# Five graphs in flight, and a layer norm whose division is moved behind the product

## The chip, the cores and the metric

One core of a Trainium2 chip runs the whole program. The metric is the device time of one launch in microseconds (us), lower is better. The runs of one kernel mostly lie within 0.3% of each other.

In this kernel TensorE multiplies and transposes matrices and writes to the memory PSUM; VectorE and ScalarE take the products out of PSUM (an eviction) and work on the memory SBUF, where GpSimd does some additions and powers too. In the lines of the profile they are PE, DVE, ACT and POOL; PEld is TensorE's loading of weights. The granted clock is the share of TensorE's full clock that the trace records.

## The reference

64 independent graphs, each with 256 nodes of 512 features and a 256x256 adjacency matrix, go through four layers. Every layer begins with the same normalisation:

```
def _layernorm(x, axis=-1, eps=1e-5):
    m = jnp.mean(x, axis=axis, keepdims=True)
    v = jnp.var(x, axis=axis, keepdims=True)
    return (x - m) / jnp.sqrt(v + eps)
# --- layer 0 (adj_preln) ---
h = jnp.maximum(_layernorm(x, axis=-1), 0.0)
x = x + _L0_gnn_ref(h, adj, L0_gnn_W_qk, L0_gnn_W_v)
# ... layers 1, 2 and 3 in the same form
```

Layer 0 multiplies h with a query/key matrix (512x128) and a value matrix (512x512). Layer 1 is a graph attention with eight heads and a masked softmax. Layer 2 is a tanh attention with eight heads. Layer 3 multiplies with a query/key matrix (512x1024), a value matrix (512x512) and the adjacency. All in float32.

The row's factor 1/sqrt(v + eps) is positive, so relu(r (x - m)) = r relu(x - m), and a product of the rows can be multiplied by r afterwards. That identity is what half of the change uses.

## The kernel before

The kernel describes each graph as some 75 tasks: what they wait for, how long each engine is estimated to need, which buffers they take and give. A planner, run once in Python while the program is built, repeatedly picks the task that could start first by its estimates and writes its instructions. So every engine's order of instructions is fixed before the chip starts. The framework below it may put instructions of one task between those of another. What the traces then show on the chip is each engine waiting for another one or for a DMA (TensorE's waits are listed in the prediction).

```
IN_FLIGHT = 4
BEHIND = 30.0
...
    def ready(self, task, ends): ...       # the estimated time at which inputs and buffers are there
    def issue(self, task, g, at):
        task.run(*[t[2] for t in passing])
        for engine, length in task.steps:
            start = max(at, self.free[engine])
            self.free[engine] = start + length
            at = start + length + (0.25 if engine == "PE" else 0.12)
    def run(self, graph, count):
        ...
                        start = max(at, self.free.get(engine, 0.0))
                        key = (round(start, 2), g.b * BEHIND - task.rest)   # the smallest is next
```

`BEHIND` weighs the number of a graph against the work that it still has to do: it decides between tasks that could start at the same time. The normalisation before:

```
@task(f"stats{layer}", after, [("V", 1.9), ("G", 0.75)])
def _():
    ...bn_stats, bn_aggr of both chunks of 128 rows...
    nc.vector.tensor_scalar(rstd, mv[:, :, 1], EPS, None, op0=OP.add)
    nc.gpsimd.tensor_tensor(rstd, rstd, power, OP.pow)
@task(f"hn{layer}", f"stats{layer}", [("V", 1.1)], {"hn": 1})
def _():
    for c in range(NC):
        nc.vector.tensor_scalar(g["hn"][:, c, :], g["xt"][:, c, :], st["mv"][:, c, 0:1],
                                st["rstd"][:, c:c + 1], op0=OP.subtract, op1=OP.mult)
# then TensorE turns each chunk, ScalarE takes it out of PSUM with a relu ("ht"), and products follow
```

In layer 1 GpSimd adds a mask to the scores of two heads (2.4 us each, 256 of them), while VectorE finds masked maxima:

```
nc.gpsimd.tensor_tensor(e, e, g["negt"][:, None].to_broadcast([P, 2, NC, N]), OP.add)
```

## Time and profile before

| | before |
|---|---|
| median time | 4856.3 us |
| TensorE / VectorE / ScalarE / GpSimd busy | 92 / 63 / 35 / 25% |
| TensorE idle, sum of the gaps ahead of its matmuls | 379 us |
| mean granted clock of TensorE | 0.961 |
| DMA share | 0.18 |

The busy shares say where the time can be won at most: only TensorE is near its limit. (The prediction speaks of 386 us of idle time: the span less the busy time. The sum of the gaps ahead of matmuls leaves out what lies after the last one, hence 379.) The waits of TensorE say what it stood for. The lines are shown in the prediction.

### The profile page before, as it was taken

The page shows a single profiled execution, that of the slowest core. Times are in us where ns is not written, and L with a number is a line of the kernel's source. Part 1 is how long each engine was busy: PE and PEld are TensorE (multiplying, and loading weights), DVE is VectorE, ACT ScalarE, POOL GpSimd, SP SyncE. Part 2 cuts the span into 40 slices and gives each one's busy share as a digit, 9 for nine tenths or more (in the row PEclk, how much of TensorE's full clock was granted, in tenths as well). Part 3 has the DMA queues.
Part 4 walks back from the last instruction along what each step waited for, and adds up shares of the span by engine and source line. Part 5 has one row for each costly group of instructions (what it writes and reads, how often), then busy time and mean ns, then how long its engine had stood idle before and what let it go on. Part 6 is the DMA issues. An engine that isn't in the chain of part 4 may idle for free.

```text
span 4848.4 us, 60906 instructions
## 1 busy us (share of the span) xinstructions
PE 4462.3 (92%) x22850; PEld 3051.0 (63%) x22850; DVE 3042.9 (63%) x7530; ACT 1679.2 (35%) x3333; POOL 1203.2 (25%) x969
## 2 busy tenths in 40 slices
PE   6799999999999999999999999999999999999998
PEld 4566666666666666666666656666666666566665
DVE  5666665666566656656666666566567656665664
ACT  1333333343343333333333333333334333333332
POOL 1231222222222212222222222122222222221220
PEclk9889999999999999999999999999999999999999
DMA  4211111111121111111111211111111112111110
GB/s 118 77 53 60 65 68 60 65 68 54 62 77 51 65 60 64 68 59 63 70 52 64 77 51 65 60 65 68 60 65 68 55 61 77 50 65 60 65 55 22
DMA packets 107975, 306.89 MB, mean 63 GB/s; under 512 B 18016, under 2 KB 48800, under 8 KB 83104
## 3 DMA queue, kind: packets, MB, share of 16 engines
q1 hardware_dynamic: 92160, 295.21, 16.9%
q10 hardware_dynamic: 15520, 7.80, 0.6%
q8 instruction: 179, 2.93, 0.3%
q14 instruction: 116, 0.95, 0.1%
HBM read 267.85 MB, written 35.13 MB: 62 GB/s over the span
## 4 chain that ended last, share of the span: by engine, by line
PE 73%; DVE 12%; issue 6%; POOL 6%; ACT 2%; DMA 1%; ACTq 0%; POOLq 0%; DVEq 0%; SPq 0%
PE tr L296 17%; PE acc L296 15%; PE acc L538 9%; PE tr L655 8%; PE tr L605 5%; PE acc L626 5%; DVE junk L477 4%; PE tr L365 4%; PE tr L677 4%; POOL pair L513 4%; PE tr L589 3%; DVE pair L608 1%; DVE hn L357 1%; PE tr L408 1%; PE tr L574 1%
## 5 line engine op out<-in xcount | busy, mean ns | idle before, releaser
L296 PE MATMUL acc<-wv_s,ht 128*128 128x512 f32 x2048 | 990.4, 627 | 31.0 <-ACT ht L366 30.8
L513 POOL TENSOR_TENSOR pair<-pair,negt 128x1024 f32<-128x1024 f32 x256 | 622.6, 2448 | 213.4 <-ACT pair L511 212.2
L296 PEld LDWEIGHTS acc<-wv_s,ht 128*128 128x128 f32 x2048 | 395.1, 203 | 436.0 <-issue 393.9
L366 ACT ACTIVATE ht<-tr 128x512 f32<-128x512 f32 x512 | 292.5, 594 | 1043.7 <-PE tr L365 940.4
L477 DVE CUSTOM_DVE_ANT_0 junk<-all,neg 128x256 f32<-128x256 f32 x1024 | 605.8, 629 | 16.7 <-DMA all<-er_d 15.8
L351 POOL TENSOR_TENSOR rstd<-rstd,power 128x2 f32<-128x2 f32 x256 | 213.1, 834 | 1326.9 <-DVE rstd L350 1026.8
L538 PEld LDWEIGHTS acc<-feats,pair 128*128 128x128 f32 x4096 | 492.4, 196 | 62.8 <-issue 48.5
L538 PE MATMUL acc<-feats,pair 128*128 128x65 f32 x4096 | 514.4, 280 | 10.7 <-ACT pair L521 10.6
L357 DVE TENSOR_SCALAR hn<-xt,mv,rstd 128x512 f32<-128x512 f32 x512 | 446.7, 900 | 110.0 <-POOL rstd L351 94.5
L549 POOL TENSOR_TENSOR xt<-xt,o 128x256 f32<-128x256 f32 x256 | 190.3, 752 | 1275.3 <-DVE o L547 1178.5
L365 PE MATMUL tr<-ident,hn 128*128 128x128 f32 x2048 | 319.7, 292 | 187.7 <-DVE feats L461 87.3
L609 ACT ACTIVATE pair<-pair 128x512 f32<-128x512 f32 x512 | 311.5, 628 | 521.1 <-DVE pair L608 520.6
L608 DVE TENSOR_TENSOR pair<-tr,at 128x512 f32<-128x512 f32 x512 | 330.9, 685 | 238.4 <-PE tr L605 231.9
L655 PE MATMUL tr<-ht,m_s 128*128 128x256 f32 x2048 | 469.3, 384 | 0.0
L296 PE MATMUL tr<-w_s,ht 128*128 128x512 f32 x1024 | 460.8, 595 | 0.8 <-ACT ht L366 0.7
L655 PEld LDWEIGHTS tr<-ht,m_s 128*128 128x128 f32 x2048 | 391.2, 193 | 84.2 <-issue 30.0
L511 ACT ACTIVATE pair<-all,ec 128x256 f32<-128x256 f32 x1024 | 426.3, 498 | 31.8 <-PE acc L538 11.8
L365 PEld LDWEIGHTS tr<-ident,hn 128*128 128x128 f32 x2048 | 252.2, 151 | 250.6 <-DVE feats L461 89.9
L521 ACT ACTIVATE pair<-pair 128x1024 f32<-128x1024 f32 x256 | 268.0, 1057 | 352.4 <-DVE pair L519 258.1
L565 DVE TENSOR_TENSOR xp<-tr,b_bc 128x512 f32<-128x512 f32 x128 | 88.2, 689 | 440.7 <-PE tr L296 440.4
L346 DVE BATCH_NORM_STATS2 stats<-xt 128x6 f32<-128x512 f32 x512 | 336.8, 677 | 16.4 <-DMA xt<-in_x_dram 10.1
L605 PE MATMUL tr<-xc,xpt 64*128 64x256 f32 x2048 | 323.3, 403 | 4.0 <-DVE xc L591 1.7
(87 smaller groups left out, 5502.0 us busy)
## 6 DMA issues: line engine op xcount, KB each, us to landing
all<-er_d SPq DMA_DIRECT2D x128, 1024.0 KB
all<-m_d SPq DMA_DIRECT2D x64, 1024.0 KB
xt<-in_x_dram SPq DMA_DIRECT2D x64, 512.0 KB
out_dram<-xt SPq DMA_DIRECT2D x64, 512.0 KB
adj<-in_adj_dram SPq DMA_DIRECT2D x64, 256.0 KB
mask_in<-in_nodemask_dram SPq DMA_DIRECT2D x64, 128.0 KB
w_n<-in_L_gnn_Wqk_dram ACTq DMA_DIRECT2D x16, 128.0 KB
wv_s<-in_L_gnn_W_v_dram ACTq DMA_DIRECT2D x1, 1024.0 KB
```

What stands on the lines that cost most here:

```text
L296: nc.tensor.matmul(p, ht[:, k, c * P:(c + 1) * P], w[:, k], start=(k == 0), stop=(k == KC - 1))
L346: nc.vector.bn_stats(stats[:, c, :], xt[:, c, :])
L357: nc.vector.tensor_scalar(g["hn"][:, c, :], g["xt"][:, c, :], st["mv"][:, c, 0:1], st["rstd"][:, c:c + 1], op0=OP.subtract, op1=OP.mult)
L365: nc.tensor.transpose(pt[:, k * P:(k + 1) * P], g["hn"][:, c, k * P:(k + 1) * P], ident)
L477: nc.vector.tensor_tensor_reduce(junk, g["all:en"][:, h, :], g["neg"][:, c, :], 1.0, -BIG, OP.add, OP.max, st["mx"][:, c, h:h + 1])
L511: nc.scalar.activation(e[:, s, j, :], g["all:es"][:, h, :], AF.Prelu, bias=st["ec"][:, j, H + h:H + h + 1], alpha=0.2)
L513: nc.gpsimd.tensor_tensor(e, e, g["negt"][:, None].to_broadcast([P, 2, NC, N]), OP.add)
L538: nc.tensor.matmul(po[i][:, h % 4, :], e[:, s, j, i * P:(i + 1) * P], feats[:, j, h, :], start=(j == 0), stop=(j == NC - 1))
L605: nc.tensor.matmul(ps[s][:, m, :], g["xpt"][half, p, m * P:(m + 1) * P], g["xc"][half, p, :], start=True, stop=True)
L608: nc.vector.tensor_tensor(th[:, s], ps[s], g["at"], OP.mult)
L609: nc.scalar.activation(th[:, s], th[:, s], AF.Tanh)
L655: nc.tensor.matmul(pz[:, s, :], m3_s[:, k, d * P:(d + 1) * P], g["ht"][:, k, :], start=(k == 0), stop=(k == KC - 1))
```

## The change

The intent: give TensorE more graphs to choose from, and shorten the chain at the head of layers 0 to 2. The statistics, the power and the normalisation are no longer in a row: a chunk is centred right after its own statistics, and the deviation divides where the products leave PSUM. To find room for a fifth graph, the adjacency has three buffers instead of four and is loaded a second time for layer 3; its transpose has five instead of four. One more constant is moved, `BEHIND` from 30 to 20.

```
-IN_FLIGHT = 4
-BEHIND = 30.0
+IN_FLIGHT = 5
+BEHIND = 20.0
-ADJ_BUFS = 4
-AT_BUFS = 4
+ADJ_BUFS = 3
+AT_BUFS = 5
...
+            late_scale = layer < 3
+            def centred(c):
+                @task(f"hn{layer}{c}", (after if late_scale else f"rstd{layer}") + ...,
+                      [("V", 1.39 if late_scale else 0.55)], {} if c else {"hn": 1})
+                def _():
+                    if late_scale:
+                        stats(c)
+                    nc.vector.tensor_scalar(g["hn"][:, c, :], g["xt"][:, c, :], mv[:, c, 0:1],
+                                            None if late_scale else st["rstd3"][:, c:c + 1], op0=OP.subtract,
+                                            **({} if late_scale else {"op1": OP.mult}))
...
-                nc.vector.tensor_copy(g["qk"][:, c, :], pq[:, :2 * A0])
+                nc.vector.tensor_scalar(g["qk"][:, c, :], pq[:, :2 * A0], st["rstd0"][:, c:c + 1], None,
+                                        op0=OP.mult)
...
-                nc.vector.tensor_tensor(g["xp"][:, c, :], pf, b2_bc, OP.add)
+                nc.vector.scalar_tensor_tensor(g["xp"][:, c, :], pf, st["rstd2"][:, c:c + 1], b2_bc,
+                                               op0=OP.mult, op1=OP.add)
... (layer 1's evictions and layer 0's weights in the same way)
-        @task("neg", "fa0", [("G", 0.7)], {"neg": 1})
+        @task("neg", "load <at", [("G", 0.7)], {"neg": 1}, {"adj": (1, 2)})
...
+        @task("again", "y0", [("D", 4.0)], {"adj": 1})
+        def _():
+            nc.sync.dma_start(g["adj"], adj[b].rearrange("(c p) m -> p c m", p=P))
```

More of the change, by code (lines that the diff above doesn't have):

```diff
@@ L328, in _ @@
             nc.sync.dma_start(g["adj"], adj[b].rearrange("(c p) m -> p c m", p=P))
-        @task("at", "load", [("PE", 0.45), ("A", 0.6)], {"at": 1}, banks=1)
+        @task("at", "load", [("PE", 0.45), ("A", 0.6)], {"at": 1}, {"adj": (1, 2)}, banks=1)
         def _(pa):
@@ L338, in normed @@
         def normed(layer, after):
-            @task(f"stats{layer}", after, [("V", 1.9), ("G", 0.75)])
-            def _():
-                xt = g["xt"]
-                stats = small.tile([P, NC, 6], F32, name="stats")
-                mv = small.tile([P, NC, 2], F32, name="mv")
-                for c in range(NC):
-                    nc.vector.bn_stats(stats[:, c, :], xt[:, c, :])
-                for c in range(NC):
-                    nc.vector.bn_aggr(mv[:, c, :], stats[:, c, :])
-                rstd = small.tile([P, NC], F32, name="rstd")
-                nc.vector.tensor_scalar(rstd, mv[:, :, 1], EPS, None, op0=OP.add)
-                nc.gpsimd.tensor_tensor(rstd, rstd, power, OP.pow)
-                st["mv"], st["rstd"] = mv, rstd
@@ L354, in _ @@
-            @task(f"hn{layer}", f"stats{layer}", [("V", 1.1)], {"hn": 1})
-            def _():
-                for c in range(NC):
-                    nc.vector.tensor_scalar(g["hn"][:, c, :], g["xt"][:, c, :], st["mv"][:, c, 0:1],
-                                            st["rstd"][:, c:c + 1], op0=OP.subtract, op1=OP.mult)
+            late_scale = layer < 3
+            def centred(c):
+                @task(f"hn{layer}{c}", (after if late_scale else f"rstd{layer}") + (f" <hn{layer}0" if c else ""),
+                      [("V", 1.39 if late_scale else 0.55)], {} if c else {"hn": 1})
+                def _():
+                    if late_scale:
+                        stats(c)
+                    mv = st[f"mv{layer}"]
+                    nc.vector.tensor_scalar(g["hn"][:, c, :], g["xt"][:, c, :], mv[:, c, 0:1],
+                                            None if late_scale else st["rstd3"][:, c:c + 1], op0=OP.subtract,
+                                            **({} if late_scale else {"op1": OP.mult}))
@@ new lines, in stats, with root @@
+            def stats(c):
+                if not c:
+                    st[f"mv{layer}"] = small.tile([P, NC, 2], F32, name="mv")
+                six = small.tile([P, 6], F32, name="six")
+                nc.vector.bn_stats(six, g["xt"][:, c, :])
+                nc.vector.bn_aggr(st[f"mv{layer}"][:, c, :], six)
+            def root():
+                st[f"rstd{layer}"] = rstd = small.tile([P, NC], F32, name="rstd")
+                nc.vector.tensor_scalar(rstd, st[f"mv{layer}"][:, :, 1], EPS, None, op0=OP.add)
+                nc.gpsimd.tensor_tensor(rstd, rstd, power, OP.pow)
@@ L360, in turned @@
+            if late_scale:
+                for c in range(NC):
+                    centred(c)
+                task(f"rstd{layer}", f"hn{layer}0 hn{layer}1", [("V", 0.18), ("G", 0.75)])(root)
+            else:
+                @task(f"rstd{layer}", after, [("V", 1.9), ("G", 0.75)])
+                def _():
+                    for c in range(NC):
+                        stats(c)
+                    root()
+                for c in range(NC):
+                    centred(c)
             def turned(c):
-                @task(f"ht{layer}{c}", f"hn{layer}" + (f" <ht{layer}0" if c else ""), [("PE", 0.5), ("A", 0.6)],
+                @task(f"ht{layer}{c}", f"hn{layer}{c}" + (f" <ht{layer}0" if c else ""), [("PE", 0.5), ("A", 0.6)],
@@ L380, in weighted @@
                 value(c)
-            @task(f"soft{layer}", after, [("PE", 0.25), ("V", 0.42), ("A", 1.0), ("V", 0.4)], banks=1)
+            @task(f"soft{layer}", after + f" rstd{layer}", [("PE", 0.25), ("V", 0.42), ("A", 1.0), ("V", 0.4)], banks=1)
             def _(pr):
                 st["w"] = softmax_nodes(pr, st["wc"])
+                if layer == 0:
+                    nc.vector.tensor_tensor(st["w"], st["w"], st["rstd0"], OP.mult)
             @task(f"add{layer}", f"soft{layer} pv{layer}0 pv{layer}1", [("V", 1.5)], {}, {"acc": NC})
@@ L393, in query @@
         def query(c):
-            @task(f"qk{c}", f"ht0{c}" + (" <qk0" if c else ""), [("PE", 0.95), ("V", 0.29)],
+            @task(f"qk{c}", f"ht0{c} rstd0" + (" <qk0" if c else ""), [("PE", 0.95), ("V", 0.29)],
                   {} if c else {"qk": 1}, {"ht": (1, 4)}, banks=1)
@@ L423, in first @@
         def first(c):
-            @task(f"fa{c}", f"ht1{c}" + (" <fa0" if c else ""), [("PE", 1.88), ("V", 0.6)],
+            @task(f"fa{c}", f"ht1{c} rstd1" + (" <fa0" if c else ""), [("PE", 1.88), ("V", 0.6)],
                   {} if c else {"feats": 1}, {"ht": (1, 4)}, banks=1)
@@ L430, in _ @@
                 rows(pf, g["ht"], c, w1a_s)
-                nc.vector.tensor_copy(st["ec"][:, c, :], pf[:, :E])
-                nc.vector.tensor_tensor(g["feats"][:, c, :HA, :U], pf[:, E:].rearrange("p (h u) -> p h u", h=HA),
-                                        b1_bc[:, :HA * U].rearrange("p (h u) -> p h u", h=HA), OP.add)
+                nc.vector.tensor_scalar(st["ec"][:, c, :], pf[:, :E], st["rstd1"][:, c:c + 1], None, op0=OP.mult)
+                nc.vector.scalar_tensor_tensor(
+                    g["feats"][:, c, :HA, :U], pf[:, E:].rearrange("p (h u) -> p h u", h=HA),
+                    st["rstd1"][:, c:c + 1], b1_bc[:, :HA * U].rearrange("p (h u) -> p h u", h=HA),
+                    op0=OP.mult, op1=OP.add)
         for c in range(NC):
@@ L456, in second @@
         def second(c):
-            @task(f"fb{c}", f"ht1{c} <fa0", [("PE", 1.74), ("V", 0.42)], {}, {"ht": (1, 4)}, banks=1)
+            @task(f"fb{c}", f"ht1{c} rstd1 <fa0", [("PE", 1.74), ("V", 0.42)], {}, {"ht": (1, 4)}, banks=1)
             def _(pf):
@@ L460, in _ @@
                 rows(pf, g["ht"], c, w1b_s)
-                nc.vector.tensor_tensor(g["feats"][:, c, HA:, :U], pf.rearrange("p (h u) -> p h u", h=H - HA),
-                                        b1_bc[:, HA * U:].rearrange("p (h u) -> p h u", h=H - HA), OP.add)
+                nc.vector.scalar_tensor_tensor(
+                    g["feats"][:, c, HA:, :U], pf.rearrange("p (h u) -> p h u", h=H - HA),
+                    st["rstd1"][:, c:c + 1], b1_bc[:, HA * U:].rearrange("p (h u) -> p h u", h=H - HA),
+                    op0=OP.mult, op1=OP.add)
         for c in range(NC):
@@ L560, in project @@
         def project(c):
-            @task(f"xp{c}", f"ht2{c}" + (" <xp0" if c else ""), [("PE", 3.47), ("V", 0.69)],
+            @task(f"xp{c}", f"ht2{c} rstd2" + (" <xp0" if c else ""), [("PE", 3.47), ("V", 0.69)],
                   {} if c else {"xp": 1}, {"ht": (1, NC)}, banks=1)
@@ L564, in _ @@
                 rows(pf, g["ht"], c, w2_s)
-                nc.vector.tensor_tensor(g["xp"][:, c, :], pf, b2_bc, OP.add)
+                nc.vector.scalar_tensor_tensor(g["xp"][:, c, :], pf, st["rstd2"][:, c:c + 1], b2_bc,
+                                               op0=OP.mult, op1=OP.add)
         for c in range(NC):
@@ L662, in graph, with _ @@
             times_m(q)
-        @task("am", "ht30", [("G", 1.3)], {"am": 1})
+        @task("again", "y0", [("D", 4.0)], {"adj": 1})
+        def _():
+            nc.sync.dma_start(g["adj"], adj[b].rearrange("(c p) m -> p c m", p=P))
+        @task("am", "again", [("G", 1.3)], {"am": 1}, {"adj": 1})
         def _():
@@ L684, in graph @@
         weighted(3, wv3_s, "score30 score31", 6)
-        @task("store", "add3", [("D", 4.0)], {}, {"xt": 1, "adj": 1})
+        @task("store", "add3", [("D", 4.0)], {}, {"xt": 1})
         def _():
```

## The prediction

> **What bounds the kernel now.** I read the page first (busy shares, clock), then the waits of TensorE, then a window table of single periods, then the timeline round its larger gaps. The page says which engine is nearest its limit:
>
> ```profile
> PE 4462.3 (92%) x22850; PEld 3051.0 (63%) x22850; DVE 3042.9 (63%) x7530; ACT 1679.2 (35%) x3333; POOL 1203.2 (25%) x969
> ```
>
> TensorE has work in 92% of the span, no other engine in more than 63%. So the change can win only what TensorE loses: 4848.4 - 4462.3 = 386 us of idle time, plus what it loses by a lower clock. The list of what TensorE waited for (total us, times, longest):
>
> ```profile
> PE tr L365 <- DVE feats L461: 87.3, 11, 8.7
> PE tr L365 <- DVE hn L357: 80.3, 24, 6.0
> PE tr L408 <- DVE qk L398: 67.8, 38, 4.2
> PE acc L296 <- ACT ht L366: 30.8, 11, 3.1
> PE tr L263 <- DMA mask_rows<-in_nodemask_dram: 25.8, 1, 25.8
> PE tr L639 <- DVE pair L608: 23.7, 9, 3.0
> ```
>
> The three largest are waits for VectorE, though VectorE is idle for a third of the time, and they come 11, 24 and 38 times, not 64: the schedule has a rhythm. The 8.70 us gap returns every 444 us, from 564.1 to 4565.1, nine periods of six graphs (the loss of several periods is the same gaps at the same places: 8.7, 3.1, 4.2, 2.5, 0.7, 0.8, 6.0 and 2.4 us). Two periods in windows:
>
> ```profile
> core 0: us, PE busy (x) PEld busy (x) DVE busy (x) ACT busy (x) POOL busy (x), PEclk, DMA share, GB/s
> 1008.50:1452.40 443.90, 413.65 (x2137) 283.18 (x2136) 283.77 (x703) 156.89 (x314) 112.55 (x91) 0.97 0.18 63
> 1452.40:1896.60 444.20, 413.71 (x2137) 283.16 (x2136) 283.42 (x703) 157.11 (x314) 112.72 (x91) 0.97 0.17 63
> ```
>
> Per period 444.2 - 413.7 = 30.5 us idle, and a mean clock of 0.97 costs about 0.03 x 444 = 13 us more. Full-speed work is therefore about 444 - 30.5 - 13 = 400 us, 66.7 us a graph; the kernel's own list of TensorE durations adds up to 66.7 too. A graph costs 74.0 us now, so 10% is the most to be had in the steady part.
>
> Why VectorE is late where it is not full: the timeline of one 4.2 us gap.
>
> ```profile
> 2055.08 0.15 DVE L350 TENSOR_SCALAR rstd<-mv 128x2 f32<-128x2 f32 x1
> ...
> 2055.31 0.70 POOL L351 TENSOR_TENSOR rstd<-rstd,power 128x2 f32<-128x2 f32 x1 [0.44 <-DVE rstd L350]
> ...
> 2055.97 4.82 POOL L513 TENSOR_TENSOR pair<-pair,negt 128x1024 f32<-128x1024 f32 x2
> 2056.05 5.03 DVE L357 TENSOR_SCALAR hn<-xt,mv,rstd 128x512 f32<-128x512 f32 x2 [0.81 <-POOL rstd L351]
> ...
> 2061.00 0.47 DVE L398 COPY qk<-tr 128x128 f32<-128x128 f32 x2
> ...
> 2061.33 1.97 PE L408 MATMUL tr<-qk,at 128*128 128x64 f32 x8 [4.23 <-DVE qk L398]
> ```
>
> VectorE makes eps + variance, GpSimd raises it to the power -0.5, and VectorE's two normalisations come after. GpSimd goes on at once with two mask additions; each normalisation then takes 2.5 us and ends with one of them. Alone it takes 0.55 us:
>
> ```profile
> L357 DVE TENSOR_SCALAR hn<-xt,mv,rstd x512: 515/545/2586, 11.7 to 4819.9; 128x512 f32<-128x512 f32 x171
> L477 DVE CUSTOM_DVE_ANT_0 junk<-all,neg x1024: 381/416/2581, 102.0 to 4731.6; 128x256 f32<-128x256 f32 x171
> ```
>
> (minimum, median, maximum ns.) The mean of the 512 normalisations is 900 ns on the page, so 512 x (0.900 - 0.545) = 182 us are stretched time; the masked maxima lose 1024 x (0.629 - 0.416) = 218 us the same way. The 8.7 us gap is such a case: four maxima of 2.55 us ahead of the eviction (line 461) that frees TensorE's bank.
>
> [...] Here, after the gap shown, the window 2061.3 to 2066 has a granted clock of 0.50. [...]
>
> **The change, part by part.**
>
> 1. *Deviation after the product (layers 0 to 2).* Chunk by chunk: statistics 0.677 + aggregation 0.164 + subtraction about 0.545 = 1.39 us, after which that chunk can be turned. Before: 2 x 0.677 + 2 x 0.164 + 0.16 + about 0.8 of power and 0.5 of waits + 0.55 = 3.7 us to the first normalised chunk when nothing blocks. About 2.3 us shorter, three times per graph, and no longer through GpSimd's queue. Power and eps addition stay, 256 each, now beside the turns and the first product. Operation counts of VectorE hardly change: copies of 128x128 (283 ns) and 128x16 (174 ns) become multiplications from PSUM, additions of a bias become one fused operation (417 ns for a fused 256-element one from PSUM, against 414 to 421 for the addition). One small multiplication is added in layer 0: 64 x about 0.2 = 13 us of VectorE, off the path.
> 2. *Less collision.* 210 of the 512 normalisations start within 0.4 us of a power's end (mean 0.96 us), the other 302 have 0.86 us; so the tie to the power is only part of it. In layers 0 to 2 (384 of them) I take the stretch from 0.36 to 0.22 us: 54 us less VectorE time in all, but what counts is the gaps: those behind a normalisation are 6.0 + 4.2 + 2.4 = 12.6 us a period, and I expect half, -6.3 us.
> 3. *Five graphs in flight instead of four.* TensorE's order is fixed when the program is built, from estimated durations, so a fifth graph offers work where four had none. It doesn't loosen the order itself: work placed just after its estimated producer is still late if that producer is stretched. I give it -7 us of the other 18 us a period. With five x buffers the fifth graph loads only when the oldest has stored, some microseconds, so it is 4.9 rather than 5.
> 4. *Clock.* [...] 13 us lost becomes about 6.5, -6.5 us. Rounding of small gaps: -2.
> 5. *Adjacency loaded twice* (three buffers, five for its transpose): 64 x 262,144 bytes = 16.8 MB on 307 MB, with the DMA share at 0.18. Hidden. The mask moves from behind the first product to just after the load: same work, earlier.
>
> Sum: -6.3 - 7 - 6.5 - 2 = about -22 us a period, 198 us in nine. The 847 us outside the nine periods have some 110 us of idle time, 36 of it the loading of weights, which stays; I take 15 us off. 4857 - 213 = 4644, so 4640.
>
> **The rivals.**
>
> *A: blocked operations stay, the gaps only move.* For it: [...] the maxima (218 us stretched) are untouched, and the 2.45 us additions are the same 256. VectorE would still be late, in other places. Against: the three waits named above lie on the shortened chain or its neighbours. Then the time stays at 4780 to 4860.
>
> *B: new waits take over.* The evictions now need the power; if GpSimd is in two additions (4.9 us), VectorE's queue stops at an eviction, and a PSUM bank with it. Three adjacency buffers and a second load in the one in-order DMA queue could hold up the masks; only two mask buffers exist and they are now held from the load on. For it: the queue already stands 2298 us in waits for the maxima's rows. Against: the power has the turns and a product, 4 us and more, to end in, and the profile has no TensorE wait for DMA after the start. It would give 4700 to 4900.
>
> *C: nearly all gaps close*, as the fifth graph fills whatever is late: 66.7 x 54 = 3602 for the steady part instead of 4001, with 847 - 30: about 4430. Against: order is fixed and VectorE's delays are not in the estimates.
>
> **Range and chances.** Between A and C, with the middle at 4640; 8 in 10 for 4500 to 4790. The bound for 2% is 4760. Faster by over 2%: 0.80; within 2%: 0.16; slower: 0.04.
>
> **What would show it.** TensorE's share 95 to 96% with the same instruction count; idle in total near 200 us; mean clock 0.98 rather than 0.961; under 72.5 us a graph in the steady part. The waits behind line 357's successor and the query's eviction at half or less; the mean of the centring operation 0.7 to 0.8 us. VectorE's busy time within 3% of before. DMA bytes up by 17 MB and no TensorE wait for one. I am wrong if the idle time stays at 350 us or more (A), or if TensorE waits for banks whose evictions wait for the power, or for the mask or the second load (B); and in size if the rhythm of gaps vanishes altogether (C).

Marked cuts in the recorded texts (here, and in what was expected of e10 and e20) took out statements on the hardware that no trace or run of this case had shown. That half of the 13 us, which stand for the measured mean clock of 0.97, goes with the gaps is a bare estimate. One of the reasons for rival A, that the subtraction alone can still be held up, went too; the traces show it only afterwards (up to 2.62 us in e1 and 2.67 in the changed kernel, where the median is 0.48).

## More of the kernel before

In layer 2 two heads of 64 rows or columns share TensorE's array. Their products are written next to each other, and each half has its own tanh:

```
for s in range(2):                                     # the two heads of a pair
    nc.vector.tensor_tensor(th[:, s], ps[s], g["at"], OP.mult)
    nc.scalar.activation(th[:, s], th[:, s], AF.Tanh)
...
for m in range(NC):
    for s in range(2):
        nc.tensor.matmul(pyt[s * U:(s + 1) * U, p % 2, :], g["xp"][:, m, h * U:(h + 1) * U],
                         g[f"pair:th{p}"][:, s, m, :], start=(m == 0), stop=(m == NC - 1))
```

## The result, and the profile after

The changed kernel takes 4772.0 us (median of 4 runs, 4769.9 to 4774.4) against 4856.3 us: a ratio of 0.9827 (95% interval 0.981 to 0.9844). A ratio is the mean time of one kernel's fast runs over that of the other's in the same rounds, so it is not quite the ratio of the medians. That is 1.7% where 4.5% was forecast.

The page's busy line of the changed kernel:

```profile
PE 4521.0 (95%) x22850; PEld 3059.4 (64%) x22850; DVE 2883.6 (60%) x7594; ACT 1701.1 (36%) x3333; POOL 1211.6 (25%) x969
```

Read it against the line of before with care. The share went from 92 to 95%, as forecast, but part of that is no gain: the same 22850 matmuls are busy for 4521 us instead of 4462, 59 us more. The waits of TensorE:

```profile
PE tr L385 <- DVE hn L351: 74.4, 33, 12.4
PE acc L654 <- ACT pair L637: 32.0, 41, 2.9
PE tr L263 <- DMA mask_rows<-in_nodemask_dram: 25.4, 1, 25.4
PE tr L519 <- DVE feats L486: 12.6, 3, 4.2
PE tr L519 <- DVE mx L517: 11.8, 6, 3.6
PE tr L278 <- DMA w_n<-in_L_gnn_Wqk_dram: 11.0, 1, 11.0
```

The waits for the query's eviction (67.8 us) and for the feature eviction ahead of the turns (87.3 us) are gone from the top. A new one stands second: products with the tanh scores wait for ScalarE's tanh (2.4 us in the kernel before). The schedule has a rhythm here too, of 1242.4 us for 17 graphs (6052 of 22850 matmuls, of which a graph has 356):

```profile
core 0: us, PE busy (x) PEld busy (x) DVE busy (x) ACT busy (x) POOL busy (x), PEclk, DMA share, GB/s
1241.60:2484.00 1242.40, 1193.41 (x6052) 807.50 (x6052) 760.65 (x2007) 450.40 (x884) 321.87 (x256) 0.98 0.19 68
```

A graph has 49.0 / 17 = 2.9 us of idle time, against 30.5 / 6 = 5.1 before, yet it takes 73.1 us against 74.0. So I split each span in three: the gaps ahead of matmuls; half of the time that TensorE was busy in stretches with a granted clock of 0.50 (what the half clock cost: in the trace of before, weight matmuls of 128x512 into `acc` start every 0.854 us in stretches at 0.50 and every 0.429 at 1.00, in the median); and the rest, TensorE's work as if it always had its full clock. (The split is counted over every instruction of the traces, time in which two matmuls overlap only once.)

| us | span | gaps | half clock | work at full clock | of it half-array products |
|---|---|---|---|---|---|
| before | 4848 | 379 | 133 | 4336 | 722 |
| changed | 4771 | 243 | 120 | 4408 | 780 |
| difference | -78 | -136 | -13 | +72 | +58 |

This is the result in one row. The gaps shrank by 136 us. The half clock shrank by 13 us only. And 72 us came back as "work", though there is not one matmul more. 58 of them are in layer 2's products that fill half of the array; the other 14 are not explained.

Why those: two of them that stand next to each other mostly run at the same time. In the trace of the kernel before, 2314 pairs of its 5120 half-array matmuls start within 0.04 us of each other. There, a whole product with the tanh scores of two heads, eight instructions, takes 1.08 us (timeline of TensorE; start, length):

```profile
2408.07 1.08 PE L626 MATMUL acc<-pair,xp 128*64 128x256 f32 x8
...
2412.28 0.65 PE L626 MATMUL acc<-pair,xp 128*64 128x256 f32 x2
2412.86 0.70 PE L605 MATMUL tr<-xc,xpt 64*128 64x256 f32 x4
2413.49 1.08 PE L626 MATMUL acc<-pair,xp 128*64 128x256 f32 x6
```

The second one was cut in two by the order of instructions: its first head alone (2 instructions, 0.65 us), something else, then the other 6 in 1.08 us. Together 1.73 us instead of 1.08. Counted over the order in the built programs, 40 of the 256 such products are cut before and 62 after; of the products with the head matrices, runs of two instructions for the same head (a sign of the same thing) rose from 9 to 53. In the traces 231 fewer pairs of half-array matmuls start together (2083 after, 2314 before), and a pair that doesn't costs one more interval of about 0.21 us, the usual distance from one pair to the next in the trace of before: an estimate of 231 x 0.21 = 49 us, most of the 58.

The half clock, in windows of the changed kernel round one of its gaps, a gap of 1.58 us from 2505.2:

```profile
2495.00:2504.00 9.00, 9.00 (x46) 5.75 (x46) 1.96 (x10) 1.51 (x5) 2.70 (x2) 1.00 0.30 117
2504.00:2507.40 3.40, 1.82 (x10) 1.28 (x10) 3.40 (x7) 1.06 (x1) 0.00 (x0) 0.99 0.00 0
2507.40:2517.60 10.20, 10.20 (x37) 6.46 (x38) 6.13 (x13) 5.03 (x10) 5.43 (x3) 0.50 0.00 0
2517.60:2527.00 9.40, 9.40 (x62) 6.58 (x58) 7.36 (x18) 5.58 (x10) 0.86 (x1) 1.00 0.01 2
```

TensorE was busy for 1.82 us of the second window's 3.4, and the next 10.2 us ran at 0.50. (The traces record the clock in steps of 3.41 us; hence the length in these counts.) Gaps of 3 us and more did fall, from 46 (278 us) to 12 (91 us), but gaps of 1.2 to 1.8 us rose from 6 to 26, and the stretches of half clock fell only from 57 to 36. In 18 of these 36 no gap that touched the 3.4 us before them was as long as 2 us; in the kernel before that held for 4 of the 57. In the 93 stretches of both, TensorE was busy for up to 2.36 us of the 3.4 us before.

### The profile page after: what moved, and what is told of

It is laid out like the page before. It is cut to its first block, busy times and chain, and to the rows that moved or that the text cites. A ratio compares the mean times of both kernels' runs of the same rounds, so it can differ in the third digit from the quotient of the medians.

```text
span 4770.8 us, 60891 instructions
## 1 busy us (share of the span) xinstructions
PE 4521.0 (95%) x22850; PEld 3059.4 (64%) x22850; DVE 2883.6 (60%) x7594; ACT 1701.1 (36%) x3333; POOL 1211.6 (25%) x969
## 4 chain that ended last, share of the span: by engine, by line
PE 79%; DVE 14%; ACT 2%; issue 2%; POOL 1%; DMA 1%; ACTq 0%; DVEq 0%; POOLq 0%; SPq 0%
PE acc L296 18%; PE tr L296 17%; PE tr L683 9%; PE acc L565 8%; PE acc L654 6%; PE tr L633 5%; PE tr L385 4%; PE tr L709 4%; DVE junk L504 3%; PE tr L617 3%; DVE hn L351 2%; DVE pair L546 2%; DVE six L359 1%; PE tr L431 1%; PE tr L667 1%
## 5 line engine op out<-in xcount | busy, mean ns | idle before, releaser
L296 PE MATMUL acc<-wv_s,ht 128*128 128x512 f32 x2048 | 948.9, 606 | 3.4 <-ACT ht L386 3.3
L296 PEld LDWEIGHTS acc<-wv_s,ht 128*128 128x128 f32 x2048 | 378.9, 194 | 405.0 <-issue 383.0
L504 DVE CUSTOM_DVE_ANT_0 junk<-all,neg 128x256 f32<-128x256 f32 x1024 | 519.6, 550 | 22.4 <-DMA all<-er_d 21.7
L538 ACT ACTIVATE pair<-all,ec 128x256 f32<-128x256 f32 x1024 | 447.9, 498 | 189.6 <-PE acc L565 93.6
L365 POOL TENSOR_TENSOR rstd<-rstd,power 128x2 f32<-128x2 f32 x256 | 229.9, 900 | 863.5 <-DVE rstd L364 807.3
L654 PE MATMUL acc<-pair,xp 128*64 128x256 f32 x2048 | 349.8, 407 | 32.7 <-ACT pair L637 32.0
L576 POOL TENSOR_TENSOR xt<-xt,o 128x256 f32<-128x256 f32 x256 | 201.5, 800 | 668.8 <-DVE o L574 548.7
L359 DVE BATCH_NORM_STATS2 six<-xt 128x6 f32<-128x512 f32 x512 | 335.1, 677 | 45.5 <-DMA xt<-in_x_dram 39.6
L546 DVE TENSOR_TENSOR pair<-pair,all 128x1024 f32<-128x1024 f32 x256 | 320.7, 1278 | 52.5 <-POOL pair L540 29.3
L633 PE MATMUL tr<-xc,xpt 64*128 64x256 f32 x2048 | 337.0, 410 | 6.3 <-DVE xp L592 3.8
```

The source lines that it names most:

```text
L296: nc.tensor.matmul(p, ht[:, k, c * P:(c + 1) * P], w[:, k], start=(k == 0), stop=(k == KC - 1))
L359: nc.vector.bn_stats(six, g["xt"][:, c, :])
L504: nc.vector.tensor_tensor_reduce(junk, g["all:en"][:, h, :], g["neg"][:, c, :], 1.0, -BIG, OP.add, OP.max, st["mx"][:, c, h:h + 1])
L538: nc.scalar.activation(e[:, s, j, :], g["all:es"][:, h, :], AF.Prelu, bias=st["ec"][:, j, H + h:H + h + 1], alpha=0.2)
L546: nc.vector.tensor_tensor(e, e, g["all:m"][:, 2 * p:2 * p + 2, None, :].to_broadcast([P, 2, NC, N]), OP.subtract)
L633: nc.tensor.matmul(ps[s][:, m, :], g["xpt"][half, p, m * P:(m + 1) * P], g["xc"][half, p, :], start=True, stop=True)
```

## The experiments

Eighteen runs, all correct except three. Theory P is the prediction's: VectorE's operations are held up by GpSimd, normalisations above all. In the trace of the kernel before, the 103 of 512 normalisations that overlap one of GpSimd's mask additions take 2.56 us in the median, the other 409 take 0.54 (0.89 at most); 84 take over 2 us, and each of these ends within 0.29 us of such an addition. That is what held up, or blocked, means below. Theory S came from the split above: an order of instructions that cuts half-array products in two. Theory L came later: an order fixed from estimates scatters so much that one order says little about a change.

### The two halves of the change, apart

**e1** keeps the plan of before, tasks and estimates included, and exchanges the arithmetic only:

```
-  tensor_scalar(hn, xt, mean, rstd, op0=subtract, op1=mult)
+  tensor_scalar(hn, xt, mean, None, op0=subtract)             # layers 0 to 2; evictions multiply
```

> The kernel before with its plan untouched (four graphs, same tasks, same estimates); only the arithmetic is the new one: layers 0 to 2 subtract the mean without waiting for the power, the evictions multiply. Theory P (my prediction's: normalisations tied to GpSimd's power make the gaps): the 12.6 us of gaps behind normalisations in a period of six graphs fall by half, the half-clock stretches behind them too, 10 us a period, so about 4756 us, and the mean of the centring operation falls from 900 to under 750 ns. Rival R (VectorE is blocked by GpSimd's additions wherever it stands): mean above 850 ns and 4840 to 4860 us.

Measured: 4820.6 us, ratio 0.9926. The time lies between the two theories. The mean of all 512 operations is 752 ns, just over Theory P's 750 (634 in the 384 of layers 0 to 2, 1105 in layer 3's 128), but the gaps fell by 25 us only and the half clock not at all (136 us). The waits of TensorE in this run say why:

```profile
PE tr L367 <- DVE feats L468: 85.6, 11, 8.5
PE tr L367 <- DVE hn L358: 73.0, 15, 6.0
PE tr L413 <- DVE qk L402: 51.7, 20, 2.8
```

The gap of 6.0 us is unmoved. It ends at

```profile
1743.42 2.30 DVE L350 TENSOR_SCALAR rstd<-mv 128x2 f32<-128x2 f32 x1
...
1745.65 1.60 POOL L351 TENSOR_TENSOR rstd<-rstd,power 128x2 f32<-128x2 f32 x2
1746.64 1.00 DVE L358 TENSOR_SCALAR hn<-xt,mv,rstd 128x512 f32<-128x512 f32 x2 [0.59 <-POOL rstd L351]
```

An operation with `rstd` among its inputs is layer 3's here, which the change leaves as it was. And what is held up is not even the normalisation but the addition of eps to 128x2 numbers, 2.30 us where it takes 0.15 alone. It ends within 0.04 us of the mask addition that GpSimd began at 1743.18 (2.50 us). So for this gap Theory P was right in what holds VectorE up, and named the wrong operation.

**e2** is the other half: five in flight with its buffers, second load, early mask and the weight of 20, and the arithmetic of before (`late_scale = False`, plain evictions; the two chunks are still normalised in two tasks).

> The changed kernel with the normalisation of before (statistics, power, then subtract and multiply in one; plain evictions), so five in flight, buffers, second load and early mask alone. If five graphs in flight bring what was measured, about 4780 us; if the late deviation brings it, 4840 to 4870. Theory S (the time lost is in pairs of half-array products that the order of instructions splits): 63 of the 256 products with the tanh scores are split in this program's order, as in the changed kernel (62), so TensorE's busy time stays at 4500 us or more whatever the idle time does.

Measured: 4738.8 us, ratio 0.9756, 33 us faster than the changed kernel. Gaps 250 us, half clock 97, work 4379. So the fifth graph with what belongs to it was worth 118 us in this order, more than the whole change, and the order already cuts the half-array products (756 us of them against 722). Theory S missed: TensorE's busy time is 4469 us, not 4500 or more.

**e3** is the changed kernel with `IN_FLIGHT = 4`.

> The changed kernel with four graphs in flight instead of five, nothing else. Its order splits 4 of 256 products with the tanh scores (62 in the changed kernel), none of the pairs with the head matrices (53) and 5 score pairs (40). Theory S: TensorE's busy time at full clock falls by about 55 us against the changed kernel, so the time is 4700 to 4740 unless the idle time grows. Theory F (five in flight closes the gaps): idle time back to 330 us or more and 4830 to 4860 us.

Measured: 5008.9 us, ratio 1.0311, slower than both. Half-array products took 642 us, the least of all eighteen runs, and the work fell by 120 us, more than Theory S said, but the gaps grew to 523 us, past what Theory F said, most of them one wait:

```profile
PE tr L602 <- DVE xp L592: 365.1, 103, 7.0
```

The turn of layer 2's projection follows its eviction by VectorE; the timeline shows that eviction in VectorE's queue behind maxima of 2.57 us and statistics of other graphs. VectorE itself stood 465 us before the transfer of the maxima's rows in this run (60 times; not among its large waits in the changed kernel); how much of its lateness comes from that is not shown. The operations are those of the changed kernel; only their order differs.

**e6** has one tanh for both heads of a pair, in the changed kernel.

```
-   nc.scalar.activation(th[:, s], th[:, s], AF.Tanh)      # in the loop over s
+   nc.scalar.activation(th, th, AF.Tanh)                   # after it
```

> The changed kernel with one tanh over both halves of a pair of heads in place of two; the products that read it are then split 4 times instead of 62. Theory S: about 0.5 us for each unsplit product, 58 x 0.5 = 29 us off TensorE's busy time, about 4745 us. Rival W (the split is only how a wait looks: the second half was not there): the busy time falls but idle time takes its place, 4765 to 4780 us.

Measured: 4751.1 us, ratio 0.9785. Half-array products fell from 780 to 747 us, gaps rose from 243 to 251, the half clock from 120 to 130. So the cuts cost about what Theory S said: the work fell by 4408 - 4374 = 34 us, nearly all of it in the half-array products (33 us on 58 products fewer cut, 0.57 us each, where the text's estimate was 0.5). But 8 us came back as gaps and 10 as half clock, so more than half of it was lost again and the time fell by 21 us only.

### Is the late division to blame for the 33 us?

**e7** takes the division into tasks from e2 (power before centring, both chunks' statistics together) and puts the new arithmetic into it. **e8** and **e9** set `BEHIND` back to 30, in the changed kernel and in e2. **e10** leaves the changed kernel's order as it is and lets GpSimd add only 16 of 256 columns of the mask, which is wrong:

```
-   nc.gpsimd.tensor_tensor(e, e, g["negt"][:, None].to_broadcast([P, 2, NC, N]), OP.add)
+   nc.gpsimd.tensor_tensor(e[:, :, :, :16], e[:, :, :, :16],
+                           g["negt"][:, None, :, :16].to_broadcast([P, 2, NC, 16]), OP.add)
```

> The kernel with five in flight and the old division into tasks (4739 us), but with the new arithmetic put into those tasks: layers 0 to 2 subtract only, evictions multiply. Theory A (the arithmetic is good, the new division into tasks by chunks is what costs the changed kernel 33 us): about 30 us less, as it was with four in flight under the old plan, so 4695 to 4720 us. Rival B (the multiplying evictions cost under five in flight, because they wait for the power): 4740 to 4775 us and VectorE waits for GpSimd's power ahead of the evictions.

> The changed kernel with the planner's weight for the age of a graph at 30 instead of 20: no operation is added or removed, only the order changes. Theory L (an order that is fixed from estimates carries a scatter of its own): the time moves by 20 us or more in either direction from 4772 us. If the order's scatter is small, 4762 to 4782 us. It splits 18 of the 256 tanh products instead of 62 and 20 pairs with the head matrices instead of 53; if splits decide, the half-array busy time falls by some 35 us and the time to about 4735 us.

> The kernel with five in flight and the old normalisation, age weight 30 instead of 20. Theory L: it moves by 20 us or more from 4739 us, and then the 33 us between it and the changed kernel cannot be put down to the late deviation. If the late deviation really costs 33 us, both kernels move alike and the old normalisation stays ahead by 20 to 45 us at this weight too.

> The changed kernel with GpSimd's mask additions cut to 16 of each 256 columns (results wrong on purpose)[...]. Theory P (VectorE is late because GpSimd blocks it): the maxima fall from 550 to under 440 ns, the centring from about 600 to 500 ns, the idle time of TensorE from 243 to under 150 us and the time to 4650 us or less. Rival O (the order itself, with pairs split and short waits, holds the rest): idle time stays above 200 us and the time above 4720 us.

Measured: e7 4667.7 us (0.9618), e8 4530.9 us (0.9336), e9 4740.8 us (0.9768), e10 4613.3 us (0.9505).

e7 suggests that the arithmetic is good under five in flight too: 71 us less than e2, more than Theory A said, with e2's tasks and estimates. But the framework's order still came out a little different (55 instead of 63 cut products), and after the scatter shown below 71 us of one order are no proof. Its rival B, evictions that wait for the power, falls: no wait of VectorE for GpSimd's power at an eviction is in its trace.

e8 is the surprise. Not one operation differs from the changed kernel, and it is 241 us faster, while e9 moved by 2 us.

e9 misses both things that its text allowed: it did not move by 20 us, and the old normalisation is 210 us behind at this weight, not ahead. Nor does it show a small scatter: against e2 its gaps grew from 250 to 331 us while the work fell from 4379 to 4324 and the half clock from 97 to 85. That these cancelled is luck. So the 33 us can't be put down to the late division.

e8's page and two of its periods (7 graphs in 481.2 us, 68.7 us a graph, 9.4 us idle, clock 0.99):

```profile
PE 4356.9 (96%) x22850; PEld 3014.1 (67%) x22850; DVE 2904.0 (64%) x7594; ACT 1671.0 (37%) x3333; POOL 1167.9 (26%) x969
```
```profile
1585.70:2066.90 481.20, 471.80 (x2492) 326.81 (x2492) 315.55 (x827) 182.18 (x364) 127.72 (x106) 0.99 0.20 72
2066.90:2548.20 481.30, 471.85 (x2493) 327.06 (x2492) 315.68 (x827) 182.08 (x364) 127.77 (x106) 0.99 0.20 72
```

The sum of e8 is 165 us of gaps, 50 of half clock, 4314 of work: of the 241 us, 94 are work (70 in half-array products, 780 to 710), 78 gaps and 70 half clock. VectorE is not held up less in it: its centring takes 745 ns in the mean against 638 in the changed kernel, its maxima 529 against 550. So it isn't the total amount of blocking that separates the two. Nor do the gaps themselves show that it falls at other places: the time by which VectorE's operations inside TensorE's gaps behind VectorE exceed their own medians is 38 us in both (counted from 130 us on, in gaps over 0.15 us).

e10 shows how much GpSimd's mask additions cost in the changed kernel: with them cut to a sixteenth and the order left alone, maxima take 440 ns, the gaps fall to 148 us, the half clock to 70, in all 159 us less. The work stays near what it was, at 4393 us, since the order still cuts the same products.

One rival is not separated: the cut also takes some 2 us out of layer 1's chain (an addition takes 0.37 instead of 2.42 us) and empties GpSimd's queue, in which the power stands. In the changed kernel's gaps VectorE stands idle for GpSimd for only 5 us, but a power that comes late while VectorE does something else would not show in that.

### How far do orders scatter?

Four runs of the changed kernel in other orders: `BEHIND = 30` with four graphs, `BEHIND = 25`, `BEHIND = 40`, and the weight of 20 with one estimate moved from 1.39 to 1.45 us. Then two of the kernel before: weight 25, and one estimate moved from 1.1 to 1.2 us. Each has two executions.

> The changed kernel with four graphs in flight and the age weight of 30, as before had it: with this the table of flight (4, 5) by normalisation (old, new) is full at weight 30: 4855 (four, old), 4741 (five, old), 4531 (five, new). If the two parts add up, 4855 - 324 + 114 = 4645 us. If the late deviation needs the fifth graph, 4800 us or more; the run with four graphs at weight 20 gave 5009 us, because VectorE's queue stood before a transfer.

> The changed kernel with age weight 25. If the weight acts in a trend (graphs kept further apart in their stages give TensorE more choice), the time lies between 4531 (30) and 4772 (20), about 4650 us. If it is scatter of single orders, it can lie outside of that stretch.

> The changed kernel with age weight 40. Trend: 4530 us or less. Scatter: anywhere from 4500 to 4800 us, then 4531 us at 30 was a lucky order.

> The changed kernel at its weight of 20, with the planner told that statistics and centring of a chunk take 1.45 us instead of 1.39; no operation differs, only the order. Scatter: over 30 us away from 4772 us in either direction. If 4772 us is what the weight of 20 gives, within 20 us of it.

> The kernel before with age weight 25 instead of 30, operations untouched. If the scatter is a property of fixed orders, 40 us or more away from 4855 us. If before was an unlucky order of its family, 4760 to 4800 us, and the change is worth less than the mean of its own orders says.

> The kernel before with the planner told 1.2 us instead of 1.1 for a normalisation, operations untouched. Same question as in the run with weight 25: 4815 to 4895 us if before is typical and its scatter small; further away if not.

| kernel, only the order differs within a row | us |
|---|---|
| four graphs, old normalisation (as before) | 4856 (weight 30), 4761 (an estimate moved), 5377 (weight 25) |
| four graphs, late division | 4777 (30), 5009 (20) |
| five graphs, old normalisation | 4739 (20), 4741 (30) |
| five graphs, late division (as changed) | 4772 (20), 4634 (20, an estimate moved), 4636 (25), 4531 (30), 4792 (40) |

Nothing in it is a trend in the weight: 40 is the slowest of the last row and 30 the fastest. With four graphs and weight 30 the late division gave 4777 us, neither the 4645 of parts that add up nor the 4800 or more of a division that needs the fifth graph. The mean of that row is (4772 + 4634 + 4636 + 4531 + 4792) / 5 = 4673 us. A change of 0.06 us in one estimate moved the time by 138 us. The three parts do not move together either: the slowest of the five (weight 40) has 352 us of gaps, 128 of half clock and only 4311 of work, the least of the row, while the changed kernel's 4408 is the most. And the kernel before was no worst case of its own row: the same operations with weight 25 took 5377 us, with two waits in nearly every graph:

```profile
PE tr L365 <- DVE low L488: 326.5, 56, 6.0
PE acc L626 <- ACT pair L609: 205.6, 60, 3.6
```

Its sum is 710 us of gaps, 329 of half clock and 4336 of work: the work is that of the kernel before, the waits are not. Line 488, a tiny operation of VectorE on 128x16 numbers, is not slow itself in this run (161 ns in the median, 487 at most). TensorE's turn simply comes too early for it in this order, and as the orders are periodic, the same 6 us come in nearly every graph (56 times in 64). The timeline of one such gap (1655.7 to 1661.7 us) shows VectorE's statistics at their usual 0.66 us, not stretched, and GpSimd's power beginning at 1660.02, when two mask additions of 4.66 us ended, 2.2 us after VectorE had added eps. So here it is GpSimd's queue, not a stretched operation of VectorE, that makes part of the wait. I have not traced this run further; it doesn't show blocking as the cause.

### Does blocking make an order bad?

**e17** and **e18** repeat the cut of e10 in the slowest and the fastest order of the changed kernel.

> The changed kernel in the order of age weight 40 (4792 us), GpSimd's mask additions cut to a sixteenth (wrong results on purpose), order unchanged. If the bad orders are those where blocked VectorE operations hit TensorE, it loses 160 us or more, as the weight of 20 did (4772 to 4613), and lands within 60 us of the same cut in the best order. If the order is bad by itself, it stays above 4700 us.

> The changed kernel in its best order (weight 30, 4531 us) with the same cut. If the good order is good because blocked operations do no harm in it, it gains little: 4480 to 4520 us. If blocking costs the same in every order, 4370 to 4400 us.

Measured: 4528.0 us (from 4792, -264) and 4420.9 us (from 4531, -110). With GpSimd's additions cut, the distance between the two orders shrinks from 261 to 107 us, and that of the weight 20 (4613) stays 192 above the best. So the large additions explain more than half of the difference between the slowest and the fastest order, but not all: e17 missed its "within 60 us of the best" by 47 us, and the order with weight 20 is held back by its 4393 us of work, 86 more than e18's 4307. That it is by holding VectorE up is supported by the gaps: the stretched time inside TensorE's gaps behind VectorE (as counted for e8) is 110 us at weight 40 and 38 at weight 30, and falls to 6 and 4 with the cut. The rival named at e10 stays open for the rest. The second rival in e18 (as much won in every order) comes nearer than my first: 110 us is little against 264, but not nearly nothing.

### A version that beats both

**e19** is e8 with the single tanh, **e20** is e8 with the mask additions on VectorE:

```
-  [("A", 2.0), ("G", 2.6)]    nc.gpsimd.tensor_tensor(e, e, negt..., OP.add)
+  [("A", 2.0), ("V", 1.2)]    nc.vector.tensor_tensor(e, e, negt..., OP.add)
```

> The changed kernel at age weight 30 with one tanh over both halves of a pair of heads. 9 split products instead of 18, so the half-array busy time falls by some 5 us and little more is there to be won; the order moves too. 4510 to 4560 us; above 4600 us it would be the scatter of orders that decides once more.

> The changed kernel at age weight 30 with the 256 mask additions on VectorE instead of GpSimd, and the planner told so (1.2 us each). VectorE gets some 256 x 1.2 = 307 us more and loses about 200 us of stretched time; it holds 66% of the span then. [...] maxima under 450 ns and 4440 to 4520 us. If VectorE's queue becomes the limit or the new order is a bad one, above 4560 us.

(The clause cut ahead of "maxima under 450 ns" was the theory that GpSimd's hold on VectorE is what is left to win.)

Measured: e19 4541.3 us (0.9351), no gain over e8. e20 4461.7 us, ratio 0.9184 (95% interval 0.9169 to 0.9198): 8.2% faster than before, 310 us faster than the changed kernel. Its busy line and its maxima:

```profile
PE 4303.5 (97%) x22850; PEld 2966.5 (67%) x22850; DVE 2929.1 (66%) x7850; ACT 1680.0 (38%) x3333; POOL 557.7 (13%) x713
```
```profile
L504 DVE CUSTOM_DVE_ANT_0 junk<-all,neg x1024: 384/422/937, 105.0 to 4333.1; 128x256 f32<-128x256 f32 x171
```

VectorE took over 256 additions and is busy for 2929 us, 25 us more than in e8: what it gained by not being held up pays for nearly all of it. The longest maximum is 0.94 us, where it was 2.62 in the changed kernel. Part of this is again a new order: of the 69 us over e8, 33 are work (half-array products 680 us against 710), so they can't all be put down to VectorE being held up less.

## Why the prediction was wrong

The measured time lies in the stated range of 4500 to 4790 us, near its slow end, but the change is -84 us where -213 was forecast. By its own steps:

- *TensorE is the bound; 386 us of idle time and a low clock are all there is to win.* The bound is right. What hid in it was wrong: "full-speed work is about 400 us a period" was taken as fixed by the count of matmuls. It is not: the same 22850 took 4336 us of full clock in the kernel before, 4408 in the changed one and 4281 in e20. **This is the step that failed.** It made +72 us out of a term that I had at zero. 58 of them are half-array products, and e6 took 33 of these back by removing one cause of the cuts.
- *Gaps: -6.3 - 7 - 2 = -15.3 us a period of six graphs.* Measured -2.2 a graph in the windows (5.1 to 2.9), or -136 us in the whole run, which is -12.8 for six of 64 graphs. Nearly right, but its parts were shared out wrongly. The fifth graph with what belongs to it took 129 us off the gaps in its one order (e2), 12.1 for six graphs where I gave it 7, and the late division 25 (e1, order held). The 6.0 us gap that I counted as the late division's belongs to layer 3, which the change leaves alone.
- *Clock: -6.5 us a period.* Measured -13 us in all, -1.3 for six graphs. **This step failed too**: that half of it would go with half of the gaps was a bare estimate, and its stretches fell from 57 to 36 only, one of them (10.2 us) right behind a gap of 1.58 us. Against -58 us in nine periods it is 45 us short; with the 72 us of work that is about 117 of the 129 us that are missing.
- *The normalisation's stretch falls from 0.36 to 0.22 us (mean 0.7 to 0.8 us in the centring).* It fell further, to 0.13. The mean of the centring alone is 634 ns in e1 and 611 in the changed kernel (subtracting alone takes 479 where nothing blocks, not 545); with layer 3's normalisations, 752 and 638. It was of little use in e1, as the blocked operation in front of the 6.0 us gap was another. From the changed kernel's table of lines:

```profile
L351 DVE TENSOR_SCALAR hn<-xt,mv 128x512 f32<-128x512 f32 x384 | 230.0, 611 | 6.2 <-PE tr L385 4.6
L351 DVE TENSOR_SCALAR hn<-xt,mv,rstd 128x512 f32<-128x512 f32 x128 | 89.1, 719 | 34.5 <-POOL rstd L365 24.8 <-PE tr L385 9.3
```

- *The evictions cost the same.* They do not: layer 2's grew from 689 to 748 ns in the mean, layer 1's from 414 and 421 to 475 and 477 (417 was forecast) and the copies from 283 and 174 to 349 and 231. There are 128 of each, 38 us of VectorE in all; whether any of it lies on the path is not shown. Layer 2's were not held up: 754 ns at most, and 752 in the 13 of 128 that overlap a mask addition.
- *Second load hidden, no new wait for DMA.* Right: 323.7 MB moved instead of 306.9, and no TensorE wait for a transfer after the start.
- *Rival B, evictions that wait for the power.* Hardly seen in the changed kernel (4.6 us ahead of one small eviction); e7 speaks against it.
- *The other signs.* TensorE idle 250 us (near 200 was forecast), mean clock 0.971 (0.98), 73.1 us a graph (under 72.5), VectorE's busy time 5% less (within 3%): all missed, none by much.
- *"Order is fixed and VectorE's delays are not in the estimates."* It was written down as a reason against rival C, and was the most important sentence: it should have widened the range instead. The changed kernel's operations in five orders span 4531 to 4792 us around a mean of 4673. That my 4640 is near the row's mean is luck; it said nothing of the one order that was measured.

What stays open: why one order is better than another beyond what was shown (GpSimd's large additions, cut products), how much of the additions' cost is VectorE held up and how much GpSimd's queue, and how much of e20's last 69 us comes from holding VectorE up less.

## What to carry to other kernels

When the order of instructions is made from estimates, compare changes over several orders, for instance by moving an irrelevant estimate a little: here that alone moved the time by 138 us, more than the change itself did. Do not take the busy time of TensorE as fixed by its instruction count: here half-array products that were cut apart (0.65 + 1.08 us instead of 1.08) and half clock behind short gaps (10.2 us at 0.50 behind one of 1.58 us) made the same matmuls longer while the busy share rose. And take the small operations into account where GpSimd's large ones run beside them: a 128x2 addition that took 2.30 us instead of 0.15 stood ahead of a gap of 6.0 us.
